# Which PSUM pair takes the sums, the gate and the next tick: a change of places behind the rounds of a two-layer convolution kernel

## The chip, the cores and the metric

The kernel runs on one core of one Trainium2 chip. The metric is device time in microseconds (us), here the median of several executions. A profile of one further execution is used to see inside; its engines are called TensorE (PE; its weight loads PEld), VectorE (DVE), ScalarE (ACT), GpSimd (POOL) and SyncE (SP, which issues nearly all DMAs).

## The reference, cut to what matters

The input is x with 8 elements of 8 channels of 512 x 512, in float32. Two layers follow one another, each with a residual:

```python
x = x + _L0_conv_ref(_gn(x), ...)   # spectral layer: a few Fourier modes of every second sample, mixed over channels, back on the full grid
x = x + _L1_conv_ref(_gn(x), ...)   # the layer below
...
for _ in range(STEPS):                                  # 15 steps
    mapped = R * grid * (1.0 - grid)
    local = _conv(mapped, K_local, groups=C_OUT)        # 3x3, each channel alone
    physics = (1.0 - EPS) * mapped + EPS * local
    grid = (1.0 - BETA) * physics + BETA * drive
cml_out = jnp.clip(grid, 0.0001, 1.0 - 0.0001)
h = jax.nn.relu(_conv(x, Wp, bp))                       # 3x3, 8 to 128 channels
nca_out = jax.nn.sigmoid(_conv(h, Wu, bu))              # 1x1, 128 to 8
gin = jnp.concatenate([x, cml_out, nca_out], axis=1)
g = jax.nn.sigmoid(_conv(jax.nn.relu(_conv(gin, Wg1, bg1)), Wg2, bg2))
return g * cml_out + (1.0 - g) * nca_out
```

`_gn` normalizes groups of two channels.

## The kernel before

**What is kept where.** Each element passes through three planes in DRAM: `xn` (the normalized input of the second layer), `cml` and `nca`. PSUM is cut into four tiles `pair0` to `pair3` of 128 x 2 x 512 floats each, two banks apiece[...]. They are never reallocated: who may write a pair next is a matter of waiting until its last reader is done.

**Ticks.** The program is one long order of work, written out by hand in `work`; every engine executes its instructions in the order of the source (`keep_order`). One call of `work` is a tick, and an element has 75 of them. In a tick, one after another:

1. Two half-steps of the 15-step map. Each convolves one set of rows (`convolve`, L536, 32 x 32 weight blocks, 48 matmuls in the source) into two pairs: the first set into `pairs[:2]`, the second into `pairs[2:]`. `settle` then adds the drive on VectorE (L591), pair by pair, and squares on ScalarE (L597). Every third step of a set its edge rows are exchanged by DMA (L566).
2. `transfers()`: DMA issues on SP for gates, halves and x.
3. None, one or two rounds of the 8-to-128 convolution (`Hidden.round`, L636): the first round into `pairs[:2]`, the second into `pairs[2:]`. Of the two pairs of a round ScalarE evicts the first (L642, relu into `h[:, :2]`) and VectorE the second (L644, into `h[:, 2:]`).
4. What comes behind the rounds, in this order on TensorE:
 - `others.first([a, ...])`: either the 3x3 convolution of a gate (`Gate.conv`, L706, into `a`, evicted by VectorE at L716), or one or two pieces of the next element's spectral layer (one piece into `a`, a second into `b` where the rounds are complete, else into `c`). A piece is, for example, the forward transform of a channel (L338, evicted by ScalarE L342), rows of the way back (L401, evicted by ScalarE L405), half a channel of the synthesis (L433, added to x by VectorE L436), or a matmul for the statistics (L305, L313; L315 reads the second).
 - If an even number of rounds is done: `Hidden.point(c)`, the sums over the 128 channels (L655, one bank of `c`), round after round, each over four blocks `h[:, g]`. They are evicted by ScalarE (L662) or added by VectorE (L664).
 - `others.second([...])`: the 1x1 part of an earlier gate (`Gate.point`, L723, evicted by ScalarE L727), or one more spectral piece, into `d` if there were sums, else into `c`.

Gates are loaded in ticks 1 to 24 of the following element and from tick 53 on; the spectral layer of the next element runs mostly from tick 24 on. The first element has no gates of an earlier one, and the four ticks ahead of it have rounds alone. Behind the last element, a tail of ticks has only rounds and gates. With two rounds in a tick the count of rounds is always even at its end, so there are always sums.

**Who takes which pair behind the rounds.** One line decides it, with one choice for ticks of one round and another for those of two or none:

```python
a, b, c, d = (pairs[i] for i in ((0, 1, 3, 2), (2, 0, 3, 2))[rounds == 1])
```

The functions touched, and what calls them:

Of the kernel before, what the change touches and what calls it, by code (L numbers as in the profile page):

```python
# [128 lines left out]
def conv_layers(ctx: ExitStack, tc: tile.TileContext, a, out):  # L129
# [27 lines left out]
    sets, shared = Slots("set", 15), Slots("shared", SHARED)  # L157
# [7 lines left out]
    pairs = [pp.tile([P, 2, N], F32, name=f"pair{i}") for i in range(4)]  # L165
# [4 lines left out]
    def later(ticks, work):  # L170
        put_off.append((now[0] + ticks, work))

    def tick(end=False):
        now[0] += 1
        due = [w for at, w in put_off if end or at <= now[0]]
        put_off[:] = [] if end else [(at, w) for at, w in put_off if at > now[0]]
        for work in due:
            work()
# [296 lines left out]
    class Half:  # L475
# [28 lines left out]
        def squares(self, n):  # L504
            for k in range(SETS):
                if k - 2 in (n, n + 1):
                    self.square(k)
# [23 lines left out]
    def convolve(m, c0, step, ps):  # L531
        for n, dx in enumerate((1, 0, 2)):
            for t in range(4):
                for h in range(4):
                    at = slice(32 * h, 32 * h + 32)
                    nc.tensor.matmul(  # L536
                        ps[h // 2][32 * t : 32 * t + 32, h % 2],
                        band[at, c0 + (t if step % 2 else h), dx],
                        m[at, t, dx : dx + N],
                        start=(n == 0), stop=(n == 2), tile_position=(32 * h, 32 * t),  # L540
                    )
# [43 lines left out]
    def settle(half, step, k, ps):  # L585

        m, d = half.m[k], half.d[k, step % 2]
        u = m[:, :, 1 : N + 1]
        for q in range(2):
            at = slice(2 * q, 2 * q + 2)  # L590
            nc.vector.scalar_tensor_tensor(  # L591
                u[:, at], ps[q], FLOOR, d[:, at], ALU.max, ALU.add
            )
            if q:
                yield
            if step < STEPS:
                nc.scalar.square(u[:, at], u[:, at])  # L597
        if step == 1:
            half.drive(k, 0)
        elif step == STEPS - 2:  # L600
            nc.gpsimd.tensor_scalar(d, d, 0.5, None, ALU.add)  # L601
        elif step >= STEPS - 1:
            sets.drop(d)
        if step == STEPS:
            leave(m, k, half)
        elif (step - k) % HALO == 0:
            later(1, lambda: renew(half.m, k, step))
# [284 lines left out]
    def work(sets, rounds, e, after, transfers, squares=lambda: None):  # L892

        settled = iter(())
        for (half, step, k), ps in zip(sets, (pairs[:2], pairs[2:])):
            convolve(half.m[k], half.c0, step - 1, ps)
            next(settled, None)
            settled = settle(half, step, k, ps)
            next(settled)
            others.finish()  # L900
        others.finish()
        transfers()
        for ps in (pairs[:2], pairs[2:])[:rounds]:
            e.hidden.round(ps, after, settled)
        next(settled, None)
        squares()

        a, b, c, d = (pairs[i] for i in ((0, 1, 3, 2), (2, 0, 3, 2))[rounds == 1])

        point = rounds and e.hidden.n % 2 == 0  # L910
        others.first([a, b if point else c])
        if point:
            e.hidden.point(c[:, 0])
        others.second([d if point else c])
        tick()
# [5 lines left out]
    for b in range(B):  # L921
# [5 lines left out]
        done, rounds = e.hidden.n, ROUNDS if after else ROUNDS_LAST  # L927
        for t in range(TICKS):
# [11 lines left out]
            def transfers():  # L940
                others.feed(t)
                for half, n in halves:
                    half.fetch(n)

            now_sets = []
            for n in (2 * t, 2 * t + 1):
                half = (e.first, e.second)[n // TICKS]
# [70 lines left out]
```

## Time and profile before

| what | value |
|---|---|
| median of 3 runs | 9907.52 us (9905.83 to 9934.52) |
| the profiled execution's own time | 9903.73 us |
| its span, first to last instruction | 9901.9 us |
| mean granted TensorE clock | 0.988 |
| TensorE matmuls, busy | 9355.4 us, 94% of the span |
| VectorE, ScalarE, GpSimd, busy | 5876.2, 4301.9, 1762.5 us |
| DMA, mean over the span | 137 GB/s |

Busy time is the sum of an engine's instruction rows. Matmuls are pipelined and their ends are modelled, so that a busy TensorE is not one at its peak; starts are what can be compared. A row of the timeline merges instructions of one line and gives the start, the duration, the engine, the line, the operation and the tiles (output before input), the count, and in brackets how long the engine had been idle and what ended that. TensorE's rows show two matmuls for each one in the source.

### The profile page before, as it was taken

What the parts mean: (1) busy time and instruction counts of PE and PEld (TensorE: products, weight loads), DVE (VectorE), ACT (ScalarE), POOL (GpSimd) and SP (SyncE); (2) the same over time, 40 slices, a digit from 0 to 9 for tenths busy, and PEclk for the clock granted to TensorE, in tenths of its full rate; (3) what the DMA queues carried; (4) which work ended last, traced back from release to release, by engine and by line L of the source; (5) the groups of instructions that cost most, each with busy time, mean ns of one, the idle gap of its engine ahead of it and who ended that gap; (6) DMA issues with size and microseconds to landing.
All of it is one profiled execution on the core that took longest, in us unless ns stands there. A gap on an engine that the chain in (4) does not pass through costs nothing. (4 is left out here: it accounts for less than half of the span.)

```text
span 9901.9 us, 353033 instructions
## 1 busy us (share of the span) xinstructions
PE 9355.4 (94%) x160496; PEld 4299.0 (43%) x160496; DVE 5876.2 (59%) x6067; ACT 4301.9 (43%) x4445; POOL 1762.5 (18%) x1406
## 2 busy tenths in 40 slices
PE   6999999999999999999999999999999999898999
PEld 3444444444444434444344444444434444444433
DVE  5665555665566655666556655566555665555655
ACT  2544444443444434444444444445444454344423
POOL 2010111103121131111312013120221202221212
PEclk9999999999999999999999999999999999999999
DMA  5241355446544465445655356652665525753688
GB/s 152 86 121 34 80 141 135 138 126 167 139 129 142 129 162 138 133 128 136 163 140 143 117 141 162 145 157 94 148 164 139 161 97 142 171 124 95 147 200 202
DMA packets 625130, 1353.61 MB, mean 137 GB/s; under 512 B 72570, under 2 KB 72698, under 8 KB 593618
## 3 DMA queue, kind: packets, MB, share of 16 engines
q1 hardware_dynamic: 621280, 1329.89, 51.3%
q8 instruction: 1261, 20.66, 0.9%
q14 instruction: 235, 1.93, 0.1%
q10 hardware_dynamic: 2354, 1.14, 0.0%
HBM read 992.42 MB, written 268.78 MB: 127 GB/s over the span
## 5 line engine op out<-in xcount | busy, mean ns | idle before, releaser
L536 PE MATMUL pair<-m,band 32*32 32x512 f32 x115200 | 4093.8, 605 | 212.5 <-issue 99.6
L597 ACT ACTIVATE m<-m 128x1024 f32<-128x1024 f32 x2240 | 2363.7, 1055 | 2812.8 <-DVE m L591 2685.0
L536 PEld LDWEIGHTS pair<-m,band 32*32 32x32 f32 x115200 | 2258.3, 103 | 1955.8 <-issue 983.1
L636 PE MATMUL pair<-cols,w_p 32*128 32x511 f32 (+1 forms) x24576 | 2862.1, 603 | 47.0 <-issue 15.9
L591 DVE SCALAR_TENSOR_TENSOR m<-pair,dO 128x1024 f32<-128x1024 f32 x1280 | 1506.5, 1219 | 1384.6 <-PE pair L536 1214.6
L636 PEld LDWEIGHTS pair<-cols,w_p 32*128 32x128 f32 x24576 | 1275.9, 186 | 1645.0 <-issue 1116.1
L591 DVE SCALAR_TENSOR_TENSOR m<-pair,dE 128x1024 f32<-128x1024 f32 x1120 | 1318.8, 1219 | 1075.4 <-PE pair L536 870.9
L644 DVE TENSOR_SCALAR h<-pair,b_p 128x1024 f32<-128x1024 f32 x1024 | 1313.0, 1283 | 812.1 <-PE pair L636 803.3
L642 ACT ACTIVATE h<-pair,b_p 128x1024 f32<-128x1024 f32 x1024 | 1141.4, 1115 | 1044.1 <-PE pair L636 1043.9
L655 PE MATMUL pair<-h,w_u 128*32 128x512 f32 x8192 | 995.0, 598 | 136.2 <-DVE h L644 124.7
L729 POOL TENSOR_TENSOR mix<-mix 96x512 f32<-96x512 f32 x344 | 438.0, 1273 | 3809.0 <-ACT mix L727 3598.7
L706 PE MATMUL pair<-gin,w_g 128*32 128x511 f32 (+1 forms) x8256 | 965.9, 601 | 31.1 <-DMA gin<-nca 17.0
L711 POOL TENSOR_TENSOR mix<-mix 96x512 f32<-96x512 f32 x344 | 446.9, 1299 | 2006.1 <-DMA mix<-nca 1276.1
L601 POOL TENSOR_SCALAR dO<-dO 128x2048 f32<-128x2048 f32 x80 | 431.9, 5411 | 1228.5 <-DVE m L591 1228.5
L655 PEld LDWEIGHTS pair<-h,w_u 128*32 128x32 f32 x8192 | 249.0, 110 | 756.7 <-issue 384.7
L706 PEld LDWEIGHTS pair<-gin,w_g 128*32 128x32 f32 x8256 | 235.8, 110 | 711.3 <-issue 471.6
L668 ACT ACTIVATE y<-y,b_u 128x512 f32<-128x512 f32 x256 | 184.7, 721 | 808.5 <-DVE y L664 808.3
L734 DVE SCALAR_TENSOR_TENSOR mix<-mix,back 96x512 f32<-96x512 f32 x344 | 327.0, 951 | 147.3 <-POOL mix L729 147.3
L662 ACT COPY y<-pair 128x512 f32<-128x512 f32 x256 | 149.8, 585 | 599.8 <-PE pair L655 490.3
L716 DVE TENSOR_SCALAR mix<-pair,b_g 128x512 f32<-128x512 f32 x344 | 257.9, 750 | 247.8 <-PE pair L706 247.8
L723 PE MATMUL pair<-mix,w_g 128*32 128x512 f32 x2064 | 356.5, 593 | 10.5 <-DVE mix L716 8.5
L529 POOL TENSOR_SCALAR dO<-dO,base 128x512 f32<-128x512 f32 x320 | 238.6, 763 | 437.1 <-DMA dO<-xn 246.3
(86 smaller groups left out, 2661.4 us busy)
## 6 DMA issues: line engine op xcount, KB each, us to landing
gin<-xn SPq DMA_DIRECT2D x344, 384.0 KB
cols<-xn SPq DMA_DIRECT2D x256, 512.0 KB
x<-in_x SPq DMA_DIRECT2D x120, 1024.0 KB
gin<-cml SPq DMA_DIRECT2D x344, 320.0 KB
gin<-nca SPq DMA_DIRECT2D x344, 320.0 KB
dE<-xn SPq DMA_DIRECT2D x320, 256.0 KB
dO<-xn SPq DMA_DIRECT2D x320, 256.0 KB
mix<-xn SPq DMA_DIRECT2D x344, 192.0 KB
```

What stands on the lines that cost most here:

```text
L536: nc.tensor.matmul(ps[h // 2][32 * t : 32 * t + 32, h % 2], band[at, c0 + (t if step % 2 else h), dx], m[at, t, dx : dx + N], start=(n == ...
L591: nc.vector.scalar_tensor_tensor(u[:, at], ps[q], FLOOR, d[:, at], ALU.max, ALU.add)
L597: nc.scalar.square(u[:, at], u[:, at])
L601: nc.gpsimd.tensor_scalar(d, d, 0.5, None, ALU.add)
L636: nc.tensor.matmul(ps[g // 2][:, g % 2, lo:hi], w_p[p, dx, i % 2], self.cols[p, i // 2, at : at + hi - lo], start=(n == 0), stop=(n == 2), ...
L642: nc.scalar.activation(h[:, :2], ps[0], AF.Relu, bias=b_p)
L644: nc.vector.tensor_scalar(h[:, 2:], ps[1], b_p, 0.0, ALU.add, ALU.max)
L655: nc.tensor.matmul(ps[32 * g : 32 * g + 32], w_u[:, r % 4], h[:, g], start=(r == self.hs[0][0]), stop=(r == self.hs[-1][0]), tile_position ...
L706: nc.tensor.matmul(ps[32 * j : 32 * j + 32, lo:hi], gband[:, dx], gin[:, j, at : at + hi - lo], start=(n == 0), stop=(n == 2), tile_positi ...
L711: nc.gpsimd.tensor_tensor(d, d, ng, ALU.subtract)
L723: nc.tensor.matmul(ps[at], gpoint[:, at], mix[:, 3], start=True, stop=True, tile_position=(0, 32 * j),)
L729: nc.gpsimd.tensor_tensor(d, d, mix[: GR * C, 2], ALU.mult)
```

## The change

In `work` the two halves of PSUM get names, `near` and `far`. For ticks with no round or with one, `a`, `b`, `c`, `d` come out as before. For ticks with two rounds, call the first round's pairs n0, n1 and the second's f0, f1:

| | a | b | c | d | next tick's first and second set |
|---|---|---|---|---|---|
| before | n0 | n1 | f1 | f0 | n0, n1 and f0, f1 |
| after | n0 | f0 | n1 | n0 | f1, f0 and n1, n0 |

The list of pairs is reversed behind each such tick, so that the next tick's first set, and its first round, go into the pairs of this tick's second round. Within a half the pairs change places too: the one that VectorE emptied comes first.

```diff
-        for (half, step, k), ps in zip(sets, (pairs[:2], pairs[2:])):
+        near, far = pairs[:2], pairs[2:]
+        for (half, step, k), ps in zip(sets, (near, far)):
             convolve(half.m[k], half.c0, step - 1, ps)
...
-        for ps in (pairs[:2], pairs[2:])[:rounds]:
+        for ps in (near, far)[:rounds]:
             e.hidden.round(ps, after, settled)
         next(settled, None)
         squares()
 
-        a, b, c, d = (pairs[i] for i in ((0, 1, 3, 2), (2, 0, 3, 2))[rounds == 1])
+        if rounds == 2:
+            (a, c), (b, _), d = near, far, near[0]
+            pairs.reverse()
+        elif rounds:
+            (a, c), (b, _), d = far, near, far[0]
+        else:
+            (a, b), (d, c) = near, far
 
         point = rounds and e.hidden.n % 2 == 0
         others.first([a, b if point else c])
```

## The prediction

> **What bounds the kernel now.** I read the page's first part, then the waits, then the timelines of TensorE, VectorE and ScalarE in single ticks.
>
> ```profile
> span 9901.9 us, 353033 instructions
> PE 9355.4 (94%) x160496; PEld 4299.0 (43%) x160496; DVE 5876.2 (59%) x6067; ACT 4301.9 (43%) x4445; POOL 1762.5 (18%) x1406
> ```
>
> TensorE is busy for 94% and nothing else comes near, so its gaps are the only time to be had. The waits (columns: total us, times, longest) name what ends them:
>
> ```profile
> PE pair L655 <- DVE h L644: 124.7, 141, 1.9
> PE pair L536 <- issue: 99.6, 59, 4.9
> PE pair L536 <- ACT m L516: 69.7, 21, 11.8
> PE pair L401 <- DVE om L393: 20.0, 8, 5.3
> ```
>
> The largest is that of the sums L655 for L644, the VectorE half of a round's eviction. The timelines of a tick with nothing between the rounds and the sums (TensorE, then VectorE, then ScalarE; start us, duration us):
>
> ```profile
> 789.45 5.43 PE L636 MATMUL pair<-cols,w_p 32*128 32x512 f32 x48
> 796.40 1.92 PE L655 MATMUL pair<-h,w_u 128*32 128x512 f32 x16 [1.52 <-DVE h L644]
> 798.25 0.84 PE L536 MATMUL pair<-m,band 32*32 32x512 f32 x16
> 794.97 1.28 DVE L644 TENSOR_SCALAR h<-pair,b_p 128x1024 f32<-128x1024 f32 x1 [1.29 <-PE pair L636]
> 794.97 1.11 ACT L642 ACTIVATE h<-pair,b_p 128x1024 f32<-128x1024 f32 x1 [0.51 <-PE pair L636]
> ```
>
> Both rounds' 48 matmuls start at 789.45. Where other work follows, it starts 5.36 later (5.25 if it is L433), so TensorE was free at 794.81 and stood until 796.40. I call the start of the rounds 0: ScalarE has evicted its half at 6.63, VectorE its own at 6.80, TensorE goes on 0.15 after that (or at 6.86 after other work). Now ticks with spectral work, then a tick with a gate (its VectorE row last):
>
> ```profile
> 1920.09 5.43 PE L636 MATMUL pair<-cols,w_p 32*128 32x512 f32 x48
> 1925.44 0.38 PE L313 MATMUL pair<-var,avg 128*128 128x1 f32 x2
> 1925.76 1.06 PE L401 MATMUL pair<-e,om 16*32 16x512 f32 x8
> 1926.94 1.92 PE L655 MATMUL pair<-h,w_u 128*32 128x512 f32 x16
> ...
> 1936.49 5.43 PE L636 MATMUL pair<-cols,w_p 32*128 32x512 f32 x48
> 1941.74 1.03 PE L433 MATMUL pair<-e,ty 8*128 8x512 f32 x4
> 1942.69 1.06 PE L401 MATMUL pair<-e,om 16*32 16x512 f32 x8
> 1943.68 1.92 PE L655 MATMUL pair<-h,w_u 128*32 128x512 f32 x16
> ...
> 5013.47 1.90 PE L655 MATMUL pair<-h,w_u 128*32 128x512 f32 x16
> 5015.19 1.03 PE L723 MATMUL pair<-mix,w_g 128*32 128x512 f32 x6
> 5013.79 0.75 DVE L716 TENSOR_SCALAR mix<-pair,b_g 128x512 f32<-128x512 f32 x1 [0.82 <-PE pair L706]
> ```
>
> In both spectral ticks L401 starts before 6.63, that is before ScalarE has emptied its half. In the gate tick L716 ends at 5014.54, 0.65 before L723 starts. L655 takes 1.72 (5013.47 to 5015.19): 16 matmuls in four steps of 0.43, eight of them for each round.
>
> [...] the first eight matmuls of L655 need only the first round's values, ready some 2 us earlier, yet wait 1.59 for the second round's VectorE eviction, whose bank they write. [...]
>
> **The change, part by part.** No instruction is added, removed or moved on any queue, DMAs included; only pairs change, and only in ticks with two rounds. Call the first round's pairs n0, n1 and the second's f0, f1 (f0 emptied by ScalarE, f1 by VectorE). I counted 406 such ticks in the TensorE timeline.
>
> 1. *Sums L655: c from f1 to n1.* The first eight matmuls wait for nothing in the second round; the other eight still need its values at 6.86. The first eight take 0.86. So:
>  - nothing ahead of the sums, 51 ticks: first half 5.36 to 6.22, the second at 6.9 instead of 7.8: 0.86 gained. In 6 of them a following L401 waits for VectorE's om anyway (the L393 row): 45 x 0.86 = 38.7.
>  - L338 ahead, 41 ticks: sums start at 5.36 + 1.06 = 6.42 instead of 6.86, and the second half no longer waits: 41 x 0.44 = 18.0.
>  - L433 alone ahead, 41 ticks: start at 5.25 + 0.95 = 6.20 instead of 6.85: 41 x 0.65 = 26.7.
>  - L305 ahead, 8 ticks: start at 5.67, first half to 6.53, the second at 6.86: 8 x 0.86 = 6.9.
>  - gate L706 ahead, 224 ticks: it takes 2.60, so the wait is over before: 0.
>  Sum: 90.3 us gained.
> 2. *Second spectral piece: b from n1 to f0.* It now waits for ScalarE's L642: 6.63 + 0.15 = 6.78. Queued behind it are the sums and everything later. L433 then L401 (22 ticks): L401 starts at 6.78 instead of 6.20, 0.58 lost, 12.8 in all. L313 then L401 (19 ticks): L401 ends at 6.78 + 0.99 = 7.77, the sums started at 6.85: 0.92 lost, 17.5 in all. Sum 30.3 lost.
> 3. *Gate's second part or last spectral piece: d from f0 to n0,* the bank of `first`. L723 must wait for L716. From the rows: L716 ends at 5014.54, release 0.15 later, a weight load of 0.11: ready at 5014.80, needed at 5015.19. It costs nothing, with 0.39 to spare; the sums are its cover, and without them L723 would stand 1.3 (1.72 - 0.39). In the 218 gate ticks with L723 behind the sums, the latest L716 ends 0.29 before L723: nothing still, barely. L433 in d behind L313 in a waits for L315, which ends 0.5 before. L305 behind L433 comes out even with VectorE's L436. I take 0; bounds 0 and +0.1 x 217 = 22.
> 4. *Halves swapped.* The next tick's first convolution L536 writes f1, f0 instead of n0, n1, so it no longer waits for L716. That wait ends 1.6 before L536 starts: gain 0. Its second convolution meets c and d as before. Unknown by any row is what the swap does to phases against the DMAs: bounds -10 and +15, taken 0.
>
> Sum: 90.3 - 30.3 = 60.0 gained on TensorE. Not all of it reaches the end: where one or two ticks later TensorE stands for a transfer or a chain on other engines, an earlier start only lengthens that stand. Such stands (L536 at 8 to 13 us instead of 6.51, L655 at 4.1) follow the prologue's four ticks (3.4), four bare ticks around the first element's transfers (3.4), nine bare ticks where elements change (7.7), six L338 ticks before L363 (2.6), three L305 ticks (2.6): 19.7; by the same rule five losses of 0.58 vanish (2.9). Absorbed: 17. **Net: 60 - 17 = 43 us.** If all overlapping stands absorb in full, it is 30; if none do, 60.
>
> The profiled execution took 9903.73 (span 9901.9 and 1.8 around it): 9860.7 after. The runs' median, 9907.52, is 3.8 above it: 9864.
>
> **Rivals.** (A) *Nothing absorbed*: 9848, or 9838 with the favourable phase. For it: most gain lies in the first element, where tick after tick repeats at 15.31 without another wait. Against: the stands above are real. (B) *Hidden anyway*: shorter ticks run into the halo transfers and gate loads, and less than 30 remains: 9880 to 9900. For: single L536 stands up to 13 us. Against: the gaining ticks mostly repeat without such a stand. (C) *Slower, by the shared bank of a and d*: L723 held by L716 in 217 gate ticks. It decides if the release comes over 0.39 later than I take it; at 0.35 beyond that it costs 76 and gives 9864 + 76 = 9940. For: the margin is small and the ticks many. Against: both durations are nearly constant. (D) *The change doesn't do what it says*: the first eight sums stay behind the second round's evictions by another wait; then part 2 alone counts, 9908 + 30 = 9938. Against: their values and their bank are free 2 us before.
>
> **How the numbers follow.** Forecast (gain 30 to 60, mostly kept) 0.62, A 0.09, B 0.20, C 0.05, D 0.04. A measurement can tell about 0.3% (30 us) from no change: faster is forecast and A, 0.71; within it B, 0.20; slower C and D, 0.09. Low end: A, 9843 between its two values. High end 9894: part of B; C, D, the rest of B and half of A stay outside. Forecast's own range 9848 to 9878.
>
> **What would show it.** The wait of L655 for L644 falls from 124.7 to about 40, its rest in bare ticks; bare ticks at 14.45 instead of 15.31; ticks of L338 at 14.78 instead of 15.22, of L433 alone at 14.57; L433 and L401 at 16.1 instead of 15.56; L313 and L401 at 17.3 instead of 16.40; gate ticks at 17.14 as now. Wrong if gate ticks lengthen, if L655 still starts at 6.95 in bare ticks, or if stands of L536 grow by what the sums gave.

## The result, and the profile after

| | before | after |
|---|---|---|
| median of 10 runs each | 9912.35 us (9901.46 to 9934.52) | 9891.79 us (9865.69 to 9899.2) |
| ratio | | 0.9978, 95% interval 0.9969 to 0.9987 |
| profiled execution, its span | 9903.73, 9901.9 us | 9872.19, 9870.4 us |
| mean granted TensorE clock, profiled execution | 0.988 | 0.985 |

The kernel is faster by 20.6 us, 0.22%, on this chip (by 10 on a second one, see the experiments); 43 us were forecast. Direction and range held, the size did not.

The page's first part, of the kernel after:

```profile
span 9870.4 us, 353295 instructions
PE 9399.0 (95%) x160496; PEld 4311.1 (44%) x160496; DVE 5874.3 (60%) x6067; ACT 4301.2 (44%) x4445; POOL 1758.2 (18%) x1406
```

The same 160496 matmuls are in both, yet TensorE's busy time rose by 43.6 us, from 9355.4 to 9399.0, and its idle time (span less busy) fell by 75.1, from 546.5 to 471.4. A part of both is bookkeeping, because the ends of matmuls are modelled. Here are a bare tick of before and one of after, both at the full clock (window, its length, busy time of TensorE, its weight loads, VectorE, ScalarE and GpSimd with their instructions, granted clock PEclk, DMA share, GB/s):

```profile
782.94:798.25 15.31, 13.79 (x258) 6.70 (x256) 7.28 (x6) 6.93 (x7) 0.00 (x0) 1.00 0.13 42
791.60:805.95 14.35, 14.09 (x259) 6.83 (x257) 7.96 (x7) 7.07 (x7) 0.00 (x0) 1.00 0.12 42
```

The same matmuls show as 0.30 us more of busy time where they are issued in two groups. Over all ticks of two rounds this makes some 14 us. Without it TensorE stands some 61 us less, about the 60 of the forecast's sum, and its matmuls take some 29 us longer. A change that takes waits away should leave the matmuls alone. The waits of TensorE (total us, times, longest):

```profile
PE pair L536 <- issue: 114.6, 71, 4.7
PE pair L536 <- ACT m L516: 82.1, 36, 13.8
PE pair L401 <- ACT h L642: 27.3, 42, 0.9
...
PE pair L655 <- ACT h L642: 17.4, 69, 0.5
...
PE pair L636 <- ACT y L662: 11.5, 2, 6.2
...
PE pair L655 <- DVE h L644: 0.5, 1, 0.5
```

The wait of the sums L655 for VectorE, 124.7 before, is gone (0.5). The new wait of L401 for ScalarE's L642 is the price counted for the second spectral piece: 27.3. L536 stands 27.4 us longer than before (15.0 for issue, 12.4 for L516). TensorE's timeline, a bare tick, then a tick with L313 and L401:

```profile
798.11 5.43 PE L636 MATMUL pair<-cols,w_p 32*128 32x512 f32 x48
803.46 1.07 PE L655 MATMUL pair<-h,w_u 128*32 128x512 f32 x8
804.79 1.22 PE L655 MATMUL pair<-h,w_u 128*32 128x512 f32 x8 [0.26 <-ACT h L642]
805.95 6.58 PE L536 MATMUL pair<-m,band 32*32 32x512 f32 x192
...
1901.17 1.06 PE L401 MATMUL pair<-e,om 16*32 16x512 f32 x8 [0.95 <-ACT h L642]
1902.16 1.92 PE L655 MATMUL pair<-h,w_u 128*32 128x512 f32 x16
...
1963.88 1.06 PE L401 MATMUL pair<-e,om 16*32 16x512 f32 x8 [0.95 <-ACT h L642]
1964.87 3.09 PE L655 MATMUL pair<-h,w_u 128*32 128x512 f32 x16
1967.90 2.10 PE L433 MATMUL pair<-e,ty 8*128 8x512 f32 x4
```

The sums now split: their first eight matmuls start the moment the rounds are issued (5.35 after 798.11), the other eight 1.33 later, and the next L536 comes 7.84 after the rounds' start where it came 8.80 (789.45 to 798.25) before. L401 waits 0.95. Both L313 ticks have that same wait; yet in the second the sums behind it take 3.09 instead of 1.92, and L433 takes 2.10 instead of 1.25. Nothing is waited for there. The stretches of these two ticks, and of the 10.2 us from 1965.9 on (columns as above):

```profile
1888.40:1905.60 17.20, 16.25 (x286) 7.76 (x270) 11.15 (x17) 9.68 (x11) 0.00 (x0) 1.00 0.15 43
1951.10:1970.30 19.20, 18.25 (x286) 7.75 (x270) 11.94 (x18) 10.41 (x12) 0.00 (x0) 0.87 0.22 77
1965.90:1976.10 10.20, 10.20 (x131) 3.74 (x137) 5.60 (x7) 2.00 (x2) 0.00 (x0) 0.52 0.81 292
```

The two ticks have equal matmuls and are 2.0 us apart, and the clock is the difference, 1.00 in the first and 0.87 in the second. So I took the clock's own record out of each trace. In these two traces it has two values, 1.0 and 0.5; in the second tick it is 0.5 from 1965.49 to 1975.73, 10.24 us. The half-speed stretches of these two traces are one to four times 3.41 us long, bar the last of each, at the kernel's end, and within a trace all of them start on one grid of 3.413 us, to within 0.02. From the start of the sums to the next L636 the second tick took 14.24 us (1964.87 to 1979.11) and the first 9.54 (1902.16 to 1911.70): the 10.24 us at half speed cost 4.70.

| half-speed stretches beginning in | before | after |
|---|---|---|
| the whole execution | 55, 239.6 us | 68, 305.4 us |
| the 19 ticks of L313 and L401 | 0 | 7, 34.1 us |
| the 6 bare ticks where L401 waits for om behind the sums | 6.8 us | 27 us |

By the 4.70 lost in 10.24 above I take the cost of half-speed time as up to half of itself, an estimate: 65.8 more of it cost up to 33, beside the 29 found above; 60 gained less 33 is 27, where the span shrank by 31.5.

### The profile page after: what moved, and what is told of

Read it like the earlier page. It is cut to its first block, busy times and chain, and to the rows that moved or that the text cites. A ratio compares the mean times of both kernels' runs of the same rounds, so it can differ in the third digit from the quotient of the medians.

```text
span 9870.4 us, 353295 instructions
## 1 busy us (share of the span) xinstructions
PE 9399.0 (95%) x160496; PEld 4311.1 (44%) x160496; DVE 5874.3 (60%) x6067; ACT 4301.2 (44%) x4445; POOL 1758.2 (18%) x1406
## 5 line engine op out<-in xcount | busy, mean ns | idle before, releaser
L536 PE MATMUL pair<-m,band 32*32 32x512 f32 x115200 | 4106.0, 605 | 236.8 <-issue 114.6
L536 PEld LDWEIGHTS pair<-m,band 32*32 32x32 f32 x115200 | 2269.0, 103 | 1983.5 <-issue 1085.0
L636 PE MATMUL pair<-cols,w_p 32*128 32x511 f32 (+1 forms) x24576 | 2862.5, 603 | 48.1 <-issue 18.7
L636 PEld LDWEIGHTS pair<-cols,w_p 32*128 32x128 f32 x24576 | 1273.4, 186 | 1648.9 <-issue 1145.8
L644 DVE TENSOR_SCALAR h<-pair,b_p 128x1024 f32<-128x1024 f32 x1024 | 1313.1, 1283 | 817.3 <-PE pair L636 813.4
L642 ACT ACTIVATE h<-pair,b_p 128x1024 f32<-128x1024 f32 x1024 | 1141.5, 1115 | 1062.1 <-PE pair L636 1052.1
L655 PE MATMUL pair<-h,w_u 128*32 128x512 f32 x8192 | 1031.0, 605 | 18.6 <-ACT h L642 17.4
L655 PEld LDWEIGHTS pair<-h,w_u 128*32 128x32 f32 x8192 | 252.5, 110 | 654.8 <-issue 356.8
L662 ACT COPY y<-pair 128x512 f32<-128x512 f32 x256 | 149.8, 585 | 573.0 <-PE pair L655 448.9
L723 PE MATMUL pair<-mix,w_g 128*32 128x512 f32 x2064 | 358.9, 593 | 6.6 <-DVE mix L716 4.7
```

The source lines that it names most:

```text
L536: nc.tensor.matmul(ps[h // 2][32 * t : 32 * t + 32, h % 2], band[at, c0 + (t if step % 2 else h), dx], m[at, t, dx : dx + N], start=(n == ...
L636: nc.tensor.matmul(ps[g // 2][:, g % 2, lo:hi], w_p[p, dx, i % 2], self.cols[p, i // 2, at : at + hi - lo], start=(n == 0), stop=(n == 2), ...
L642: nc.scalar.activation(h[:, :2], ps[0], AF.Relu, bias=b_p)
L644: nc.vector.tensor_scalar(h[:, 2:], ps[1], b_p, 0.0, ALU.add, ALU.max)
L655: nc.tensor.matmul(ps[32 * g : 32 * g + 32], w_u[:, r % 4], h[:, g], start=(r == self.hs[0][0]), stop=(r == self.hs[-1][0]), tile_position ...
L723: nc.tensor.matmul(ps[at], gpoint[:, at], mix[:, 3], start=True, stop=True, tile_position=(0, 32 * j),)
```

## The experiments

There are two theories of where the other half of the gain went. In the expectations K is the clock: where L401 now stands, the clock halves, and what follows runs slowly. S is stands: transfers or other engines take back what TensorE saved. All kernels compute the whole output; a filler is matmuls into a bank that is idle at that point, and nothing reads it. The kernel before, measured beside them, had medians of 9909 to 9911 us.

**The changed kernel once more**, with nothing edited.

> The changed kernel once more, so that the others have it beside them on one chip. Two theories for the missing half of the forecast. S (stands): TensorE saves what was summed, but more than the 17 us taken is lost in stands for transfers and for other engines. K (clock): the granted clock of TensorE halves for stretches of 3.4 us and more; the profile has 305 us of them instead of 240, and what they cost (up to half of the 66 us more) is what is missing. Both: 15 to 32 us faster than before, clock 0.982 to 0.985; K: the clock of the kernel before in its runs is higher, 0.986 to 0.988.

Measured: 9899.5 us, ratio 0.9992 (0.9983 to 1.0002), with a mean clock of 0.982 over its runs against 0.987 of the kernel before. In its profile (span 9912.8, clock 0.981) 77 stretches made 370.4 us of half speed, 68.3 of it begun in 13 of the 19 L313 ticks. On this chip the gain was 10 us only, less than the 15 to 32 expected, and its interval includes no gain at all. The profile with more half speed is the longer one: 130.8 us more of it than before cost up to 65, and 60 - 65 = -5, where its span is 10.9 longer than that of before.

**The stand of L401 filled.** In the 19 L313 ticks four sums of the first round, which nothing reads, go ahead of L401 into the idle second bank of n1. They fit into the stand.

```diff
...
         def over_rows(c):
             ps = one()
+            if spare[0] and c % 2 and c > 1:
+                to, h = spare[0]
+                for g in range(4):
+                    nc.tensor.matmul(
+                        to[32 * g : 32 * g + 32], w_u[:, 0], h[:, g],
+                        start=True, stop=True, tile_position=(0, 32 * g),
+                    )
...
+        spare[0] = (c[:, 1], e.hidden.hs[0][1]) if rounds == 2 else None
         others.first([a, b if point else c])
+        spare[0] = None
...
```

> As the changed kernel, but in the 19 ticks with L313 and L401 behind two rounds TensorE has something to do while L401 waits for ScalarE: four sums in the source (eight matmuls, 0.86 us) of the first round's values into the idle bank of n1, which nothing reads. The wait stays as it is. S: same time as the changed kernel, within 5 us. K: the half-clock stretches of these ticks (34 us in the profile after, none before) vanish, their mean falls from 17.8 to 17.3, and the whole is 10 to 17 us faster than the changed kernel, with a clock higher by 0.001 to 0.002.

Measured: 9880.95 us, ratio 0.9963 (0.9951 to 0.9976), clock 0.984. Work was added and the kernel is 18.6 us faster than the unfilled one on the same chip (9899.5), intervals apart. The timeline of such a tick, where L403 is the filler and the lines behind it are 7 higher (L408 is L401, L662 the sums):

```profile
1978.13 0.38 PE L313 MATMUL pair<-var,avg 128*128 128x1 f32 x2
1978.45 1.06 PE L403 MATMUL pair<-h,w_u 128*32 128x512 f32 x8
1979.46 1.06 PE L408 MATMUL pair<-e,om 16*32 16x512 f32 x8
1980.45 1.92 PE L662 MATMUL pair<-h,w_u 128*32 128x512 f32 x16
```

The stretch of this whole tick, in the columns of before:

```profile
1966.35:1983.57 17.22, 17.22 (x291) 7.79 (x300) 11.16 (x17) 10.02 (x11) 0.00 (x0) 1.00 0.13 37
```

L401 starts 1.33 behind L313, as without the filler, and the tick takes 17.22, as an undisturbed one of the kernel after. All 19 such ticks take 17.22 to 17.25, and no half-speed stretch begins in any. The gain of 18.6 is a little above the 10 to 17 expected. S, by which the filler changes nothing, is out for these ticks.

**Is it the standing, or how little is computed?** Two more fillers in the same 19 ticks: one as long, but of L401's own shape, 16 rows deep, and one of the 128-row sums at a quarter of the width. The edits against the filled kernel:

```diff
...
-    to[32 * g : 32 * g + 32], w_u[:, 0], h[:, g],
+    to[32 * g : 32 * g + 32], om[:, c : c + 4].rearrange("p c k -> p (c k)"), e1,
...
-    to[32 * g : 32 * g + 32], w_u[:, 0], h[:, g],
+    to[32 * g : 32 * g + 32, : N // 4], w_u[:, 0], h[:, g, : N // 4],
```

> As the filled kernel (19 ticks, work of 0.86 us that nothing reads, ahead of L401 behind L313), but with matmuls of L401's own shape, 16 rows deep instead of 128. K has two forms. K1, the clock falls where TensorE stands: these ticks are at 17.22 in all cases and the time is as the filled kernel's, 9881. K2, the clock falls where little of the array is in use: the half-clock stretches stay (30 to 70 us in these ticks) and the time is as the changed kernel's, 9900.

> As the filled kernel, but the unread work is a quarter as wide (128 columns instead of 512), some 0.2 of 0.9 us. K: part of the half-clock stretches of these ticks stay, the time lies between the filled kernel (9881) and the changed one (9900). S: as the changed kernel.

The 16-row filler: 9898.04 us, ratio 0.9986 (0.9979 to 0.9992), clock 0.983, no better than no filler (0.9992). Its timeline, L403 again the filler:

```profile
1965.15 1.06 PE L403 MATMUL pair<-e,om 16*32 16x512 f32 x8
1966.17 1.06 PE L408 MATMUL pair<-e,om 16*32 16x512 f32 x8
1967.16 3.33 PE L662 MATMUL pair<-h,w_u 128*32 128x512 f32 x16
```

and the stretch of the tick:

```profile
1953.40:1972.16 18.76, 18.76 (x294) 8.04 (x278) 12.07 (x18) 10.39 (x12) 0.00 (x0) 0.91 0.18 69
```

TensorE never stands here, and the clock falls all the same: 9 stretches, 64.9 us, in the 19 ticks. The quarter-width filler: 9866.05 us, ratio 0.9953 (0.9941 to 0.9966), clock 0.985. Its timeline:

```profile
1971.96 0.42 PE L403 MATMUL pair<-h,w_u 128*32 128x128 f32 x8
1972.98 0.63 PE L408 MATMUL pair<-e,om 16*32 16x512 f32 x4 [0.59 <-ACT h L649]
```

It takes 0.42 us and L401 still stands 0.59, yet all 19 ticks take 17.22 or 17.23 and no stretch begins in them. I had expected something between the full filler and none; a quarter is enough. So in these ticks standing alone is not what counts; a little work 128 rows deep does. Depth and operands were changed together (om and e1 for h), so which of the two matters is open. The median is 15 us below that of the full filler, but on another chip, and the intervals of the two ratios overlap, so no difference between the two is shown.

**All such stands filled.** The full filler as above; one of half the width in the 22 ticks of L433 and L401; and twelve sums in the six om ticks, behind the sums.

```diff
...
+            if spare[0]:
+                to, h = spare[0]
+                width = N if c % 2 and c > 1 or not c else N // 2
+                for g in range(4 if c else 12):
+                    nc.tensor.matmul(
+                        to[32 * (g % 4) : 32 * (g % 4) + 32, :width], w_u[:, 0], h[:, g % 4, :width],
+                        start=True, stop=True, tile_position=(0, 32 * (g % 4)),
+                    )
...
+        spare[0] = (far[1][:, 1], h) if rounds == 2 else None
         others.second([d if point else c])
+        spare[0] = None
...
```

> As the filled kernel, and TensorE is also given work that nothing reads ahead of L401 behind L433 (four sums of half width, 0.43 us, 22 ticks) and ahead of L401 behind the sums, where it waits for om (twelve sums, 2.6 us, 6 ticks). No wait is taken away. S: as the changed kernel, 9900. K: the half-clock stretches of these 28 ticks vanish too (27 to 61 us in the profiles of the changed kernel), 5 to 15 us faster than the filled kernel: 9866 to 9876, a gain of 34 to 44 on the kernel before, which is the forecast's 43.

Measured: 9852.23 us, ratio 0.9944 (0.9931 to 0.9958). The clock of its runs is 0.9875 in the mean, the kernel before's 0.9872 beside it; half speed is 250.4 us. At equal clock the change with its fillers gives 58.5 us, with 42 to 68 in the interval; I had summed 60. This version beats both kernels, and by more than was expected of it. The clock's record shows where the fillers worked. Here are the half-speed stretches that begin within 3.41 us behind the start of L401, in ticks of two rounds, one profile of each kernel:

| kernel | 19 ticks of L313, L401 | 22 ticks of L433, L401 |
|---|---|---|
| before (no stand) | 0 | 0 |
| after | 7 | 3 |
| after, again | 13 | 5 |
| stand filled, L313 ticks alone | 0 | 6 |
| quarter filler, L313 ticks alone | 0 | 6 |
| 16-row filler, L313 ticks alone | 9 | 4 |
| all stands filled | 0 | 0 |

The L433 ticks, where L401 stands 0.41, repeat what the L313 ticks show: the stretches come with the stand and go with the filler of deep matmuls. In the om ticks 6.8 us of half speed are left, all of it begun ahead of the rounds.

**The second piece without the rest.** The kernel before, with only b moved to f0.

```diff
+        if rounds == 2:
+            b = pairs[2]
```

> The kernel before with one part of the change alone: in ticks of two rounds the second spectral piece goes to f0 and waits for ScalarE. S: the 41 ticks lose the 30 us counted, 9940. K: 45 to 65 us slower, 9955 to 9975, with more half-clock stretches and a clock 0.002 to 0.004 lower than before.

Measured: 9963.81 us, ratio 1.0055 (1.0039 to 1.0072), 53 us slower, clock 0.984. From the waits of its TensorE:

```profile
PE pair L401 <- ACT h L642: 27.3, 42, 0.9
```

The wait is what I counted (30.3 lost). The other 23 are of the size of the clock's fall from 0.9872 to 0.9842, where 0.003 x 9900 are 30 us, an estimate. In the profile 11 stretches, 44.4 us, begin behind L401 in the L313 ticks, and 6 more, 20.5 us, behind L401 in the L433 ticks, where the kernel before has none of either; its half speed is 69.0 us above that of before in all.

**Other places for the second piece.** Three tries to get rid of the wait instead of filling it: b in a bank of n1, beside the sums in the other; the second piece behind the sums, in n1's second bank; the same, in n0 or f0 (the third try has `(b, d)` where the second has `(c[:, 1:2], d)`, which is a choice of two places by the kind of piece, and it tests the kind in another way).

```diff
...
-            (a, c), (b, _), d = near, far, near[0]
+            (a, c), b, d = near, near[1], near[0]
...
-            e.hidden.point(c[:, 0])
+            e.hidden.point(c[:, int(rounds == 2)])
...
```

> The second spectral piece goes to the first bank of n1 instead of f0, and the sums to the second bank of n1. So neither waits for the second round's evictions: the 30 us that L401 was counted to lose in 41 ticks are undone, and in 19 of them a further 0.2 is gained: 34 us faster than the changed kernel by S; ticks of L433 and L401 at 15.56 instead of 16.04, of L313 and L401 at 16.2 instead of 17.22. K: 44 to 51 faster, as the half-clock stretches of these ticks go too.

```diff
...
-        others.first([a, b if point else c])
+        others.first([a] if rounds == 2 else [a, b if point else c])
...
-        others.second([d if point else c])
+        others.second([(c[:, 1:2], d), d] if rounds == 2 else [d if point else c])
...
```

> As the changed kernel, but in ticks of two rounds only the first spectral piece stands ahead of the sums; what was the second piece comes behind them, in the second bank of n1 (a synthesis piece in n0). The loss of 30 us is undone, and 19 x 0.86 + 22 x 0.65 = 31 us of the same gain as in the other ticks come on top: 61 us faster than the changed kernel by S, 71 to 78 by K. Ticks of L313, sums, L401, L433 at 15.6, of L433, sums, L401 at 15.0.

> As the kernel with the sums first, but nothing behind the sums shares a pair with them: behind L433 the piece L401 goes to n0, behind L313 to f0. Ticks of L433, sums, L401 at 15.1 instead of 16.04 (22 of them, 21 us). Ticks of L313, sums, L401, L433 at 15.9 where ScalarE is free, up to 17.3 where its sigmoid L668 stands ahead of L405 and the next L536 waits for that (19 ticks, 13 us). By S 34 us faster than the changed kernel. By K 45 to 55 faster, as TensorE no longer stands ahead of L401.

Measured: 9948.6 us (1.0034, 1.0021 to 1.0047), 10029.57 (1.0116, 1.0100 to 1.0131) and 9926.77 (1.0023, 1.0015 to 1.0031); all three expectations failed. From the timeline of the first, the sums behind L401 in an L313 tick:

```profile
1918.67 3.48 PE L655 MATMUL pair<-h,w_u 128*32 128x512 f32 x16 [2.01 <-ACT ty L405]
```

and of the second, where L401 comes behind the sums:

```profile
1927.86 0.63 PE L401 MATMUL pair<-e,om 16*32 16x512 f32 x4 [1.77 <-DVE y L664]
```

L401 and the sums share a pair but no bank, and still the second user waits for the eviction of the first, 2.01 and 1.77: in both programs the order went by the pair, not by the bank. In the first the sums are held 2.01 by L405, and behind that stand they take 3.48 instead of 1.92, with a clock of 0.91 over the tick. In the third the ticks aimed at came out right (16.52 with L313, 14.95 to 15.05 to the end of L401 without), but TensorE stood elsewhere: L433 24.2 us for L405, 3.6 in the kernel after, and L536 for the exchange of edge rows (third try; no such wait is listed after):

```profile
PE pair L536 <- DMA m<-m: 22.9, 5, 5.2
```

Its half speed was 386.9 us. So three re-orderings that look better tick by tick have medians 27 to 130 us above that of the kernel after.

**No swap.** The kernel after without `pairs.reverse()`, in a single execution.

```diff
-            pairs.reverse()
```

> As the changed kernel, but the halves keep their places. The next tick's L536 then writes the pairs of the sums and of d: in 217 gate ticks it waits about 1.0 for ScalarE's L727 behind L723, in bare ticks about 1.0 for the eviction of the sums, which eats the 0.9 gained there. Both theories: gate ticks at 18.1, bare ticks at 15.3, 10100 to 10160.

Measured: 10302.79 us, more than expected. The start of the tick behind a gate tick, from the timeline:

```profile
4086.65 1.92 PE L536 MATMUL pair<-m,band 32*32 32x512 f32 x49 [1.29 <-ACT mix L727]
```

The next tick's first convolution now writes the pairs that the gate's second part and the sums have just filled, and stands 0.84 or 1.29 for their eviction: the 217 gate ticks alone are 237 us longer than in the profile of the kernel after. So the swap is what makes c = n1 and d = n0 free; what it does to the kernel alone was not tried. The rest of the 400 us was not divided further; the profile has 367.3 us of half speed.

## Why the prediction was right or wrong

**Step 1, the sums: right.** Bare ticks take 14.35 to 14.42 (14.45 written down), L338 ticks 14.78 (14.78), L433 alone 14.56 to 14.61 (14.57). The wait for L644 fell further than the 40 written down, to 0.5: the second round's sums begin with the half that ScalarE evicts. Those on VectorE's half start 0.17 later in the bare tick shown, while the first still run, so that TensorE is not idle for them and the rest of the wait is put down to L642 (17.4).

**Step 2, the second piece: the wait right, its cost too small.** L433 and L401 take 16.04 (16.1), L313 and L401 17.22 (17.3) where the clock is full. But in the profile the 19 L313 ticks became 27.2 longer in all, not 17.5: behind 0.95 us of standing and a 16-row L401 the clock fell to 0.5 in 7 of these ticks, for 34.1 us. I had read the granted clock, 0.988, and made nothing of it.

**Step 3, the gate: right.** Gate ticks take 17.14, as before; L723 starts 1.72 behind the sums. **Step 4, the swap:** taken 0, and not run alone. One wait goes with the new places: in two ticks with no convolution ahead of the rounds, L636 stands 11.5 us in all for the eviction of the sums (L662), 0.6 before, since the next second round now writes n1 first. In one of the two 5.6 stood before too, for L727. Rivals C and D did not happen: gate ticks did not lengthen, and the first sums of a bare tick start 5.35 behind the rounds, as counted.

**The sum: here it failed.** "Absorbed: 17. Net: 60 - 17 = 43 us" asked only which stands would eat an earlier start. The term left out is the clock, and it was the larger. Of the 65.8 us of half speed that the profile after has more, 44.3 begin behind an L401 that stands, and 20 in the om ticks. A thousandth of the clock is some 10 us here (0.001 x 9900, an estimate). Mean time of the runs times their mean clock removes it, roughly, as it treats all of the time as stretching with the clock, stands included:

| kernel | clock, and of before beside it | time x clock, less that of before |
|---|---|---|
| after, again | 0.9819, 0.9871 | -59 us |
| stand filled | 0.9836, 0.9871 | -65 |
| 16-row filler | 0.9826, 0.9869 | -56 |
| quarter filler | 0.9852, 0.9869 | -58 |
| all stands filled | 0.9875, 0.9872 | -51 |
| second piece alone | 0.9842, 0.9872 | +25 |

Five kernels from 10 to 58 us faster by the watch are 51 to 65 faster by this measure, around the 60 of the sum; the one that has only the loss is 25 slower, counted at 30. The three other places and the kernel without the swap, which have further stands of their own, are left out. The ten runs after have a mean clock of 0.9827; against 0.987, which the kernel before has in its runs beside the experiments, the term is 0.0043 x 9900 = 43 us, and 60 - 43 = 17 is about the 20.6 measured. So rival A, nothing absorbed, is near to what TensorE saved, and rival B named about the right time (9880 to 9900), but filling the stands of L401 won back what it puts down to transfers. How much was absorbed stays open. Some was: the prologue's four ticks, from their first round to the first L536 behind them, took 39.7 us before and 42.2 after, so the 3.4 gained there are gone. And the interval of 42 to 68 at equal clock just reaches 43. But the 27.4 us by which L536 stands longer can't count in full beside the clock, since 60 - 33 - 27 = 0 where the span shrank by 31.5; in the profile of the quarter filler the same two waits grew by 22.7, and its span is 45.4 below that of before. With all stands filled they are 174.6 in all, only 5.3 above before, though nothing was done about them.

## What to carry to other kernels

Where TensorE is the bound, read the granted clock before and after, and count a new stand twice: for its wait, and for what the clock may do to the matmuls behind it. Here this was seen where stands of 0.41 and 0.95 us lie next to matmuls of 8 and 16 rows. Busy time that rises with the same instruction count is a sign, though a part of it can be the way ends of matmuls are modelled; the clock's record decides. If such a stand can't be removed, a few matmuls that nothing reads, deep and short, in a bank idle anyway, may be cheaper than a new order of the work.

## What the runs showed of the hardware

Behind stands of 0.95 us at L401 the clock fell from 1.0 to 0.5 in 7 and 13 of the 19 ticks of two profiles, and in 9 of 19 with the 16-row filler, where TensorE does not stand at all. In the om ticks the sums end sooner and TensorE stands longer for om (24.4 us in all, 20.0 before); half speed there rose from 6.8 us to 27 and, in the second profile, 41. That the clock follows how much deep work TensorE does would fit all fillers (half-speed stretches behind L401 in 0, 0 and 9 of the 19 ticks with the full, the quarter and the 16-row one). That is my guess from these three fillers and not shown: depth and operands were changed together, and how much deep work it takes was not measured.
